# Attention steps levelled: projections in parts, score products chained, statistics spread, in a fused attention and top-p expert kernel

## The chip, the cores and the metric

One core of one Trainium2 chip runs the kernel. The metric is the device time of one execution in microseconds (us). Three executions of the kernel before were timed, and one more was profiled. TensorE multiplies matrices, VectorE and ScalarE work on rows of 128 partitions, GpSimd (POOL in the profile) does row work too and issues some of the DMAs, SyncE (SP) issues the others. "PEld" is TensorE's loading of weights. L557 is line 557 of the kernel before.

## What is computed

The input is 16 sequences of 256 tokens with 256 features. Each token is normalized; the result goes into 16-head attention (head size 16, rotary embedding, causal mask) and into eight experts, of which each token keeps those with the largest probabilities up to a sum of 0.9. Both results are added to the input.

```python
xn = layernorm(x)                                   # no scale, no shift
qkv = xn @ w_qkv.T + b_qkv;  q, k = rope(q), rope(k)
attn = softmax(where(causal, q @ k.T / 4, lowest)) @ v
p = softmax(xn @ router_w.T);  w = kept_top_p(p, 0.9)
ffn = sum_e( (silu(xn @ gate_w[e].T) * (xn @ up_w[e].T)) @ down_w[e].T * w[:, e] )
return x + attn + ffn
```

## The kernel before

All is in float32, and the work is in two stages with one order on TensorE.

**Attention stage.** A sequence is two tiles of 128 tokens. Its preparation consists of `prep_norm` (L419: normalize one tile on ScalarE, store it to `rows` in HBM through SyncE's queue, transpose it with two TensorE matmuls into `xnt`, copy to `xnT` on ScalarE), `prep_proj` (L434: matmuls `pq` for q and k and `pv` for v and the router's logits; VectorE adds the biases and does the rotary products in five operations at L445, L454, L465 to L467; GpSimd adds the halves into `qp` and `kp`, L468 and L471) and `prep_turn` (L475: four transposes of q or of k into `qt` or `kt`, then a ScalarE copy to `qT` or `kT`). Heads stand four to a group of 128 partitions, 32 partitions each, so that a product of one head uses 32 rows of TensorE.

The loop at L674 goes over steps. A step is two heads of one sequence, so that a sequence has eight steps (`PPS`), and there are 128. Step i makes the following:

- `products` (L532): the scores `s` of step i (queries by keys) and the transposed scores `st` of step i - 11 (`LAG`), each in two parts of two heads. Both write into buffers of the pool `ps_sc`, which has three in turn; `s` is allotted first.
- `probabilities` (L590): four mask matmuls into `st`, then one exponential on ScalarE (`pr`, L599), which empties the buffer of `st`.
- `maxima` (L564): four VectorE operations that reduce `s` to row maxima `top`, which empties the buffer of `s`. After the last step of a sequence `turn` transposes these and GpSimd adds them to `qT` (L588), where `st` of that sequence uses them.
- one job of the generator `prep_seq` (L639): one tile's norm, one tile's projection with rotation, or one transpose, in the order norm, norm, projection, projection, k, q, k, q.
- one tile of layer-norm sums (L399, L400) until all 32 are done, and at steps 7 and 31 `statistics` for the tiles that follow (square root on ScalarE, then two VectorE operations).
- from step 5 of every second sequence, six parts of the router for four tiles (L488), one in each step.
- every second step `weigh` (matmuls `o` of probabilities and v, copied to `oT` on ScalarE) and in the step after it `finish` (transposes `ot`, two VectorE operations, the sum into `xs` on GpSimd).

Everything that isn't a score goes through `ps_m`, a pool of two one-bank PSUM buffers in turn. Each engine runs its own queue in order. The order in the queue is not the order of the text: a scheduler makes it when the program is built, by priorities, and an instruction may stand ahead of others whose text came first. `issue_after` fixes that one instruction stands behind another.

**Before the loop** both sequences 0 and 1 are normalized and projected, and sequence 0 is turned. **After the loop** the experts run in groups of three blocks of tokens: gather by token number (L363), `expand`, `product`, and a scatter that adds into `out` (L809), both DMAs on GpSimd's queue. A ninth entry of the work, e = E, handles the block that didn't fit. `zero_fill` (L222), in step 24, clears the spare rows of `rows` and of `out` that unfilled places point to.

Of the kernel before, what the change touches and what calls it, by code (L numbers as in the profile page):

```python
# [30 lines left out]
def kernel(  # L31
# [68 lines left out]
    nc.vector.tensor_copy(ident_h, ident)  # L100
# [37 lines left out]
    for s in range(2):  # L138
# [4 lines left out]
    nc.gpsimd.memset(before, 1.0)  # L143
    nc.gpsimd.affine_select(
        before, before, pattern=[[1, E], [-1, E]], compare_op=ALU.is_gt, fill=0.0,
        base=0, channel_multiplier=0,
    )
    place = const.tile([P, E, E], F32, name="place")
    for k in range(E):
        nc.gpsimd.memset(place[:, k, :], float(k))  # L150
# [23 lines left out]
    zeros = const.tile([P, D + E], F32, name="zeros")  # L174

# [46 lines left out]
    def zero_fill():  # L222

        nc.gpsimd.memset(zeros, 0.0)
        nc.gpsimd.dma_start(
            rows[NT * P :, :].rearrange("(n p) c -> p n c", p=P),
            zeros.unsqueeze(1).to_broadcast([P, NB, D + E]),
        )
        nc.gpsimd.dma_start(
            out[NT * P :, :].rearrange("(n p) c -> p n c", p=P),  # L230
            zeros[:, :D].unsqueeze(1).to_broadcast([P, NB, D]),
        )
# [156 lines left out]
    with tc.tile_pool(name="prep", bufs=2) as prep, tc.tile_pool(  # L389
# [21 lines left out]
        seqs, stored, sums = {}, {}, {}  # L411
# [7 lines left out]
        def prep_norm(b, qi):  # L419

            t = b * NQ + qi
            xnT = seqs[b][3]
            xn = prep.tile([P, D], F32, tag="xn", name=f"xn_{t}", bufs=6)
            nc.scalar.activation(
                xn, xs[:, t, :], AF.Identity, bias=nmr[:, t : t + 1],
                scale=rstd[:, t : t + 1],
            )
            stored[b] = nc.sync.dma_start(rt[:, t, :D], xn)
            tp = ps_m.tile([P, DC, P], F32, tag="m", name=f"xnt_{t}")
            for c in range(DC):  # L430
                nc.tensor.transpose(tp[:, c, :], xn[:, ts(c, P)], ident)
            nc.scalar.copy(xnT[:, :, ts(qi, P)], tp)  # L432

        def prep_proj(b, qi):  # L434
# [12 lines left out]
            )  # L447
            pv = ps_m.tile([P, D + E], F32, tag="m", name=f"pv_{t}")
            for c in range(DC):
# [11 lines left out]

            cos = rope_sb[:, qi, 0, :].unsqueeze(1).to_broadcast([P, 2 * H, HD])
# [3 lines left out]
            nc.vector.tensor_tensor(rot[:, :, HF:], qk[:, :, :HF], sin[:, :, HF:], ALU.mult)  # L466
            nc.vector.tensor_tensor(qk, qk, cos, ALU.mult)  # L467
            nc.gpsimd.tensor_tensor(  # L468
                qp[b % 2][qi][:, :, :HD], qk[:, :H, :], rot[:, :H, :], ALU.add
            )  # L470
            sums[t] = nc.gpsimd.tensor_tensor(  # L471
                kp[b % 2][qi][:, :, :HD], qk[:, H:, :], rot[:, H:, :], ALU.add
# [59 lines left out]
        def products(now, late):  # L532
# [3 lines left out]
            for step, by_key in ((now, False), (late, True)):  # L536
                if step is None:
                    made.append(None)
                    continue
                b, c, p = step  # L540
                qT, kT, _, _ = seqs[b]
                sc = ps_sc.tile(
                    [P, 2, 512], F32, tag="sc", name=f"{'st' if by_key else 's'}_{b}_{c}_{p}"
                )
                made.append((kT if by_key else qT, qT if by_key else kT, c, p, sc, by_key))


            for first in (True, False):
                for left, right, c, p, sc, by_key in filter(None, made):
# [5 lines left out]
                    for j in range(2):  # L555
                        rows = slice(32 * (2 * p + j), 32 * (2 * p + j) + 32)
                        nc.tensor.matmul(  # L557
                            sc[:, j, to], left[rows, c, lhs],
                            right[rows, c, lhs if first else slice(0, S)],
                            start=first, stop=False, skip_group_check=True,  # L560
                        )
            return [m and m[4] for m in made]
# [76 lines left out]
        def prep_seq(b, turns_only=False):  # L639
            if not turns_only:  # L640
                for qi in range(NQ):
                    yield lambda qi=qi: prep_norm(b, qi)
                for qi in range(NQ):
                    yield lambda qi=qi: prep_proj(b, qi)
            for qi in range(NQ):
                yield lambda qi=qi: prep_turn(b, qi, "k")
                yield lambda qi=qi: prep_turn(b, qi, "q")
# [5 lines left out]
        stat_jobs = {7: (4, 8), 31: (12, 20)}  # L653
        stat_next = 2 * NQ

        for b in range(2):
            open_seq(b)
            for qi in range(NQ):
                prep_norm(b, qi)
            if b == 0:  # L660
                for qi in range(NQ):
                    prep_proj(b, qi)
        for qi in range(NQ):
            prep_proj(1, qi)
            prep_turn(0, qi, "k")
            prep_turn(0, qi, "q")
        with tc.issue_after(sums[2 * NQ - 1].ins):
            dispatch_constants()
# [4 lines left out]
        prs, jobs, held, todo = {}, None, {}, []  # L673
        for i in range(len(steps) + LAG + 5):  # L674
            if i < len(steps):
                b, c, p = steps[i]
                if i % PPS == 0 and b + 1 < B:
                    if b > 0:
                        open_seq(b + 1)
                    jobs = prep_seq(b + 1, turns_only=b == 0)  # L680
# [7 lines left out]
            if i < len(steps):  # L688
                behind = maxima(b, c, p, sc)
                if jobs is not None:  # L690
                    job = next(jobs, None)
                    if job is not None:
# [248 lines left out]
```

## Time and profile before

| | |
|---|---|
| median of three executions | 989.16 us (987.61 to 990.87) |
| the profiled execution | 983.91 us |
| its span, first to last instruction | 982.2 us |
| first matmul, first score product, first `st` | 6.80, 24.46, 48.31 us |
| step 12, step 120 begin | 52.16, 391.12 us |
| the last `st` burst begins | 435.48 us |
| mean granted TensorE clock | 0.984 |

The page gives each engine's busy time and share of the span, then the same in 40 equal slices in tenths, with the TensorE clock that was granted (PEclk, 9 is full). The list of waits says who waited for whom: the total in us, how often, and the longest. The instructions in order of time give start, duration, engine, line, and tiles as out<-in; a note in brackets is idle time before it and what ended it. Matmuls are pipelined, so they overlap in that list and their durations can't be added: the time that one takes up is from its start to the start of the next. In a table of stretches the columns are length, then busy us and number of instructions for PE, PEld, VectorE, ScalarE and GpSimd, then the granted clock, DMA share and GB/s.

### The profile page before, as it was taken

The page shows a single profiled execution, that of the slowest core. Times are in us where ns is not written, and L with a number is a line of the kernel's source. Part 1 is how long each engine was busy: PE and PEld are TensorE (multiplying, and loading weights), DVE is VectorE, ACT ScalarE, POOL GpSimd, SP SyncE. Part 2 cuts the span into 40 slices and gives each one's busy share as a digit, 9 for nine tenths or more (in the row PEclk, how much of TensorE's full clock was granted, in tenths as well). Part 3 has the DMA queues.
Part 4 walks back from the last instruction along what each step waited for, and adds up shares of the span by engine and source line. Part 5 has one row for each costly group of instructions (what it writes and reads, how often), then busy time and mean ns, then how long its engine had stood idle before and what let it go on. Part 6 is the DMA issues. An engine that isn't in the chain of part 4 may idle for free. (4 is left out here: it accounts for less than half of the span.)

```text
span 982.2 us, 17387 instructions
## 1 busy us (share of the span) xinstructions
PE 935.5 (95%) x6564; PEld 619.4 (63%) x6564; DVE 445.3 (45%) x2036; ACT 316.9 (32%) x617; POOL 393.7 (40%) x473
## 2 busy tenths in 40 slices
PE   6899999999999999899999999999999999999994
PEld 3555656565656565556676766766767677667673
DVE  6888676767676767825111244332111111121210
ACT  2544644444444443352222222222222222222221
POOL 6324333232323232424544444534544545546432
PEclk9799999999999999999999999999999999999997
DMA  7124100000020000102344242343433524335222
GB/s 242 42 69 154 44 18 27 21 23 24 23 82 23 13 12 13 44 14 56 54 94 74 44 114 34 55 102 55 91 67 49 119 45 91 69 54 95 41 27 28
DMA packets 46365, 57.53 MB, mean 59 GB/s; under 512 B 9312, under 2 KB 37600, under 8 KB 46272
## 3 DMA queue, kind: packets, MB, share of 16 engines
q0 software_dynamic: 19360, 29.81, 17.6%
q1 hardware_dynamic: 26912, 26.52, 8.5%
q8 instruction: 54, 0.88, 0.4%
q14 instruction: 39, 0.32, 0.1%
HBM read 32.14 MB, written 24.17 MB: 57 GB/s over the span
## 5 line engine op out<-in xcount | busy, mean ns | idle before, releaser
L809 POOL DMA_INDIRECT out<-ys,tokens x96 | 152.2, 1585 | 239.6 <-ACT ys L803 186.5
L763 DVE TENSOR_TENSOR hT<-act,gu 128x384 f32<-128x384 f32 (+2 forms) x132 | 69.9, 530 | 333.5 <-ACT act L762 333.5
L757 PE MATMUL gu<-xT,wg 128*128 128x384 f32 (+1 forms) x512 | 182.6, 479 | 1.4 <-DVE hT L763 1.0
L798 PE MATMUL py<-wd,hT 128*128 128x256 f32 (+1 forms) x768 | 182.4, 380 | 0.0
L570 DVE CUSTOM_DVE_ANT_0 junk<-s,mask 128x128 f32<-128x128 f32 (+1 forms) x512 | 152.9, 352 | 63.3 <-PE s L557 63.2
L757 PE MATMUL gu<-xT,wu 128*128 128x384 f32 (+1 forms) x512 | 179.8, 474 | 0.0
L798 PEld LDWEIGHTS py<-wd,hT 128*128 128x128 f32 (+1 forms) x768 | 141.7, 186 | 41.6 <-issue 3.8
L762 ACT ACTIVATE act<-gu 128x384 f32<-128x384 f32 (+2 forms) x132 | 62.2, 471 | 285.2 <-PE gu L757 285.2
L599 ACT ACTIVATE pr<-st 128x768 f32<-128x768 f32 x128 | 103.8, 811 | 154.9 <-PE st L594 154.9
L557 PE MATMUL s<-kT,qT 32*128 32x128 f32 (+1 forms) x1024 | 136.5, 366 | 3.7 <-DVE top L570 2.8
L557 PE MATMUL st<-qT,kT 32*128 32x128 f32 (+1 forms) x1024 | 125.3, 354 | 14.6 <-DVE top L570 11.8
L757 PEld LDWEIGHTS gu<-xT,wu 128*128 128x128 f32 x512 | 97.8, 191 | 61.5 <-issue 1.1
L757 PEld LDWEIGHTS gu<-xT,wg 128*128 128x128 f32 x512 | 89.8, 191 | 40.8 <-DVE hT L763 2.7
L363 POOL DMA_INDIRECT xg<-rows,tokens x96 | 94.2, 982 | 40.5 <-issue 20.4
L557 PEld LDWEIGHTS s<-kT,qT 32*128 32x128 f32 x1024 | 73.7, 188 | 33.6 <-issue 20.7
L557 PEld LDWEIGHTS st<-qT,kT 32*128 32x128 f32 x1024 | 69.2, 185 | 26.8 <-DVE top L570 22.4
L803 ACT ACTIVATE ys<-py,xg 128x256 f32<-128x256 f32 x96 | 45.4, 473 | 120.9 <-PE py L798 118.5
L630 POOL TENSOR_TENSOR xs<-xs,at 128x128 f32<-128x128 f32 x64 | 29.1, 455 | 128.4 <-DVE at L626 128.4
L468 POOL TENSOR_TENSOR qp<-qk,rot 128x256 f32<-128x256 f32 x32 | 23.5, 734 | 120.5 <-DVE qk L467 117.5
L440 PE MATMUL pq<-wqkv_sb,xnT 128*128 128x512 f32 x128 | 64.9, 631 | 0.0
L588 POOL TENSOR_TENSOR qT<-qT,topT 128x256 f32<-128x256 f32 x64 | 45.3, 739 | 41.5 <-ACT topT L586 41.5
L609 PE MATMUL o<-pr,va 128*32 128x256 f32 (+1 forms) x1024 | 58.1, 337 | 2.4 <-ACT xnT L432 0.6
(156 smaller groups left out, 916.6 us busy)
## 6 DMA issues: line engine op xcount, KB each, us to landing
rows<-xn SPq DMA_DIRECT2D x32, 128.0 KB, 1.8
wg<-in_wg SPq DMA_DIRECT2D x8, 512.0 KB, 4.0
wu<-in_wu SPq DMA_DIRECT2D x8, 512.0 KB, 5.0
wd<-in_wd SPq DMA_DIRECT2D x8, 512.0 KB, 3.9
out<-xs SPq DMA_DIRECT2D x16, 256.0 KB, 2.4
xs<-in_x SPq DMA_DIRECT2D x3, 1024.0 KB, 12.1
rows<-zeros POOLq DMA_DIRECT2D x1, 1716.0 KB, 8.1
out<-zeros POOLq DMA_DIRECT2D x1, 1664.0 KB, 12.4
```

The source lines that it names most:

```text
L363: nc.gpsimd.indirect_dma_start(out=xg[:n, :], out_offset=None, in_=rows, in_offset=bass.IndirectOffsetOnAxis(ap=token, axis=0),)
L440: nc.tensor.matmul(pq, xnT[:, c, ts(qi, P)], wqkv_sb[:, c, : 2 * D], start=(c == 0), stop=(c == DC - 1),)
L557: nc.tensor.matmul(sc[:, j, to], left[rows, c, lhs], right[rows, c, lhs if first else slice(0, S)], start=first, stop=False, skip_group_ch ...
L570: ins = nc.vector.tensor_tensor_reduce(junk[:, : hi - lo], sc[:, j, lo:hi], mask[:, 2 * P - (hi - lo) :], -1.0, -MASKED, ALU.add, ALU.min, ...
L599: nc.scalar.activation(pr, sc[:, :, :W], AF.Exp)
L609: nc.tensor.matmul(o[32 * hh : 32 * hh + 32, kc * P :], v[:, kc, 4 * c + hh, :], pr[:, j, : 2 * P] if kc == 0 else pr[:, j, 2 * P :], star ...
L757: nc.tensor.matmul(gu[:, j, :w], w_sb[:, c, ts(i, P)], xT[:, c, :w], start=(c == 0), stop=(c == DC - 1),)
L762: nc.scalar.activation(act[:, :w], gu[:, 0, :w], AF.Silu)
L763: nc.vector.tensor_tensor(hT[:, i, :w], act[:, :w], gu[:, 1, :w], ALU.mult)
L798: nc.tensor.matmul(py[:n, :], hT[:, i, k * P : k * P + n], d_sb[:, i, :], start=(i == 0), stop=(i == IC - 1),)
L803: nc.scalar.activation(ys[:n, :], py[:n, :], AF.Copy, scale=weights_of(e, xg, n))
L809: ins = nc.gpsimd.indirect_dma_start(out=out, out_offset=bass.IndirectOffsetOnAxis(ap=token, axis=0), in_=ys[:n, :], in_offset=None, compu ...
```

## The change

- `products` allots the buffer of `st` (the late step) ahead of that of `s`, and puts `st` ahead in each part. Every matmul of the burst but the first gets a higher priority and `issue_after` its forerunner.
- `prep_norm` handles both tiles of a sequence at once, with one PSUM tile and one copy. `prep_proj` is split into `prep_qk`, `prep_v` and `rotation`, which is a generator of two parts and does the k sum ahead of the q sum. A table `prep_jobs` says what each of the eight steps does: transposes and matmuls, and how many parts of rotations. Norm of a sequence is the last step two sequences ahead.
- Before the loop only sequence 0 is projected in full; sequence 1 has its norm and its first q and k projection there, and the rest in steps 0 to 7.
- One tile of layer-norm sums in every second step; `statistics` at steps 6, 22 and 54.
- The router's constants are made after the first kp and qp sums. The half-precision identity is copied by ScalarE instead of VectorE. `zero_fill` leaves out the last block of `out`; that one is cleared in the last entry of the expert work, behind a scatter of the last expert.

```diff
-    nc.vector.tensor_copy(ident_h, ident)
+    nc.scalar.copy(ident_h, ident)
...
-            for step, by_key in ((now, False), (late, True)):
+            for step, by_key in ((late, True), (now, False)):
...
-                        nc.tensor.matmul(
-                            sc[:, j, to], left[rows, c, lhs],
-                            right[rows, c, lhs if first else slice(0, S)],
-                            start=first, stop=False, skip_group_check=True,
-                        )
+                        with ExitStack() as hold:
+                            if opened is not None:
+                                hold.enter_context(tc.high_priority(offset=400))
+                                hold.enter_context(tc.issue_after(opened.ins))
+                            opened = nc.tensor.matmul(
+                                sc[:, j, to], left[rows, c, lhs],
+                                right[rows, c, lhs if first else slice(0, S)],
+                                start=first, stop=False, skip_group_check=True,
+                            )
...
-        def prep_norm(b, qi):
+        def prep_norm(b):
...
+            tp = ps_m.tile([P, NQ, DC, P], F32, tag="m", name=f"xnt_{b}")
+            for qi in range(NQ):
...
+            nc.scalar.copy(
+                xnT.rearrange("p c (q t) -> p q c t", q=NQ), tp
+            )
...
+        def rotation():
+            t, qk = unturned.pop(0)
...
             nc.vector.tensor_tensor(rot[:, :, :HF], qk[:, :, HF:], sin[:, :, :HF], ALU.mult)
             nc.vector.tensor_tensor(rot[:, :, HF:], qk[:, :, :HF], sin[:, :, HF:], ALU.mult)
+            yield
             nc.vector.tensor_tensor(qk, qk, cos, ALU.mult)
+            sums[t] = nc.gpsimd.tensor_tensor(
+                kp[b % 2][qi][:, :, :HD], qk[:, H:, :], rot[:, H:, :], ALU.add
+            )
             nc.gpsimd.tensor_tensor(
                 qp[b % 2][qi][:, :, :HD], qk[:, :H, :], rot[:, :H, :], ALU.add
             )
-            sums[t] = nc.gpsimd.tensor_tensor(
-                kp[b % 2][qi][:, :, :HD], qk[:, H:, :], rot[:, H:, :], ALU.add
-            )
...
+        def prep_jobs(b):
...
+            jobs = [
+                ([lambda: prep_qk(b, 0)] if b > 1 else [], 0),
+                ([lambda: prep_v(b, 0)], 1),
+                ([lambda: prep_qk(b, 1)], 1),
+                ([lambda: prep_v(b, 1)], 1),
+                (turn_of(0, "k"), 1),
+                (turn_of(0, "q") + turn_of(1, "k"), 0),
+                (turn_of(1, "q"), 0),
+                ([norm] if b + 1 < B else [], 0),
+            ]
...
-        stat_jobs = {7: (4, 8), 31: (12, 20)}
+        stat_jobs = {6: (4, 4), 22: (8, 8), 54: (16, 16)}
...
-                if jobs is not None:
-                    job = next(jobs, None)
-                    if job is not None:
-                        job()
+                todo_now, parts_now = jobs[i % PPS]
                 with tc.issue_after(behind.ins):
-                    if stat_next < NT:
+                    for _ in range(parts_now):
+                        if turning is None:
+                            turning = rotation()
+                        if next(turning, 0) == 0:
+                            turning = None
+                for job in todo_now:
+                    job()
...
+                with tc.issue_after(behind.ins):
+                    if stat_next < NT and i % 2 == 0:
...
-                        zero_fill()
+                        nc.gpsimd.memset(zeros, 0.0)
+                        zero_fill(rows, 0, NB)
+                        zero_fill(out, 0, NB - 1)
...
+                if e == E:
+                    with tc.issue_after(added[E - 1][-1]):
+                        ins = zero_fill(out, NB - 1, NB)
+                    for other in sum(added.values(), [])[:-1]:
+                        tc.declare_no_dep(ins.ins, other, reason="other rows")
+                    added[E - 1].append(ins.ins)
```

## The prediction, made before the changed kernel was run

> **What bounds the kernel now.** I read the page's busy shares, then the waits, then TensorE's instructions in order of time, step by step through the attention half, then two stretches that are one sequence each.
>
> ```profile
> PE 935.5 (95%) x6564; PEld 619.4 (63%) x6564; DVE 445.3 (45%) x2036; ACT 316.9 (32%) x617; POOL 393.7 (40%) x473
> PEclk9799999999999999999999999999999999999997
> ```
>
> TensorE is busy 95% of 982.2 us, so the end is set by what stands in its queue, and a gain has to show there. From about 450 us on (the experts) its order does not change. What can move lies in the first 440 us, and most of it inside what counts as busy.
>
> ```profile
> 200.91 0.38 PE L557 MATMUL s<-kT,qT 32*128 32x128 f32 x2
> 200.92 0.38 PE L557 MATMUL st<-qT,kT 32*128 32x128 f32 x2
> ...
> 201.77 0.40 PE L594 MATMUL st<-maskT_h,ident_h 128*128 128x128 bf16 x4
> ...
> 209.80 0.38 PE L557 MATMUL s<-kT,qT 32*128 32x128 f32 x2
> ...
> 233.78 0.49 PE L557 MATMUL s<-kT,qT 32*128 32x128 f32 x4
> 235.42 0.38 PE L557 MATMUL st<-qT,kT 32*128 32x128 f32 x2 [1.15 <-DVE top L570]
> 236.28 0.40 PE L594 MATMUL st<-maskT_h,ident_h 128*128 128x128 bf16 x4
> ```
>
> A step has a burst of sixteen 32-row matmuls: eight for s (step i) and eight for st (step i-11). The two use different 32-row groups. When both are ready they start together (first two lines) and the burst takes 201.77 - 200.91 = 0.86 us. Where eight run alone at the end of the stage (418.36 to 419.21) they take 0.85 us too: st is free if it is there in time. In the last three lines s runs alone, st comes 1.64 us late, and the burst takes 2.50 us.
>
> ```profile
> PEld st L557 <- DVE top L570: 22.4, 42, 1.7
> PE st L557 <- DVE top L570: 11.8, 16, 1.5
> 197.56:221.53 23.97, 23.64 (x271) 14.97 (x271) 16.06 (x85) 11.70 (x21) 7.40 (x12) 1.00 0.07 24
> 221.53:247.70 26.17, 24.32 (x271) 15.26 (x271) 19.40 (x98) 11.81 (x22) 7.40 (x12) 1.00 0.08 23
> ```
>
> The releaser of st is the maxima on VectorE: with three score buffers and s allotted first, st takes the buffer that s of the step before had, and waits for its four maxima. The two stretches are eight steps each, without and with the router (VectorE 16.06 and 19.40 us). Their eight bursts, from first score product to masks with foreign matmuls taken out, take 9.24 us (0.87, 0.87, 1.08, 1.03, 0.87, 1.43, 1.65, 1.44) and 11.42 us; whole they would be 8 x 0.87 = 6.95. So 2.29 and 4.47 us a sequence are lost, and the rest is the same in both: 23.97 - 2.29 = 21.68, and 26.16 - 4.47 = 21.69 (step 59 to 67 and on to 75). From step 12 (52.16 us) to step 120 (391.12) lie 13.5 sequences: 338.96 us, 25.1 each, 3.43 of them lost, 46 us in all.
>
> **The change, part by part.**
>
> *Late products allotted first, bursts chained.* By the allocation order st now takes the buffer of s two steps back, whose maxima are mostly long done: the wait above goes. What is late next: s takes the buffer of st of the step before, so s waits for that step's exponential on ScalarE. In the trace the exponential starts 0.43 us after the first mask matmul (421.41 to 421.84), takes 0.81, and TensorE follows a ScalarE copy about 0.06 later (26.15 to 26.21): s can start 1.30 us after its predecessor's masks begin. Masks hold TensorE for 0.23, so 1.07 us of other matmuls must stand between masks and the next burst. No row shows this wait; the nearest are late st: 0.23 late cost 1.08 - 0.87 = 0.21, 0.36 cost 0.56, 0.58 cost 0.57. I take these.
>
> *Preparation in parts.* No matmul is added or removed; they are spread. In the built order, with start-to-start times from the same stretch (pq 1.77, pv 0.95, o 0.79, kt 0.5, qt 0.44, four xnt 0.44, ot 0.33, top 0.32), what follows the masks is by step of the sequence: 0: pq, top 2.09. 1: pv, ot 1.28. 2: pq, o 2.56. 3: pv, ot 1.28. 4: kt, o 1.29. 5: qt, kt 0.94. 6: qt 0.44 (ot moved ahead of the masks). 7: xnt, ot 0.77 (o ahead of the masks). So steps 0 to 4 cover the exponential, barely in 1, 3 and 4 (0.2 us). After 5, s is 0.13 late: 0.2. After 6, 0.63: 0.6. After 7, 0.30, and the copy of o (0.37) stands ahead of the exponential, so about 0.49: 0.55. Sum 1.35, sequence 21.68 + 1.35 = 23.0.
>
> *The router sequence.* In step 3 the reductions r_m, r_p, the exponential on ScalarE and four more operations (1.4 us from 231.79 to 233.16, then 0.34) now stand on VectorE behind maxima, rotation half and v bias, and ahead of step 4's maxima and of the last rotation product. VectorE's queue, summed from step 2: step 3's maxima to 2.2 us after that burst begins, rotation and v 1.1, rs, at and router 1.9, step 4's maxima 1.2, product 0.6, then GpSimd's kp add 0.73: kp of the second tile comes 7.7 us, with the hand-overs some 7.9, after step 3's burst began, against 6.3 at which TensorE reaches its transpose in step 5. TensorE waits 1.6 us there, which covers step 5's 0.2. Behind that transpose stand step 6's burst and all else. Sequence 21.68 + 1.6 + 0.6 + 0.55 = 24.4. Bounds: 0.2 (VectorE catches up) to 3. Step 3's router exponential also stands ahead of step 4's on ScalarE; that 0.3 us lies within the 1.6.
>
> Gain per pair of sequences: (23.97 - 23.0) + (26.16 - 24.4) = 2.7; times 6.75 pairs, -18.2 us.
>
> *Statistics spread out.* VectorE has one tile in every second step instead of one in each (0.42 + 0.18 us busy): less in the first 24 steps, the same sum. But statistics now come at steps 6, 22 and 54, and 22 and 54 come just one step before the norm that needs them: square root, two VectorE operations, two norms (0.6 each), transposes, copy, then pq, with the next exponential between. The built order has three pairs of changes between the tables of square root and exponential after the start where there were two. Row: each load is 1.28 us (39.78, 47.54), so 2.6 for the added pair. The Trainium skill (ScalarE: Activation LUTs, What ACT_TABLE_LOAD costs) gives about 1283 ns for the load, which agrees, and about as much again for a drain, 2.66 in all, hence 5.3. The existing pair in step 33 lengthened its burst from 1.65 to 2.27 us only, since ScalarE is half idle. I take 2 us for each of 22 and 54, bounds 0 and 4: +4.
>
> *The start.* The first score product no longer stands behind pq and pv of sequence 1's second tile, its first pv and its first transposes. Before, it starts at 24.46 and its maxima at 26.96. By the same rows qT and kT of sequence 0 are ready near 22.6, so maxima start about 3.5 us earlier; 4.2 us of rotation and bias enter VectorE's queue in the eleven s-only steps and 2.6 of statistics leave. Then xnt, two pq and pv stand ahead of the first st, as one did before. I get step 12 at 49.4 instead of 52.16: -2.8, bounds -5 and +1; the upper depends on the clock, 0.5 from 36.5 to 46.7 us here. The cast of ident_h (5.30 us on VectorE at 5.94, beside GpSimd's fills) goes to ScalarE between norm and copy, where TensorE is waiting for nothing shorter: 0; uncovered it would be about 0.3. Router constants leave GpSimd's queue ahead of the first qp and stand behind kp and qp of sequence 0: 0, they are needed steps later. kp now goes ahead of qp: kT is used first, 0.
>
> *Joined xnT copies* (one instead of two): 0.2 us of ScalarE a sequence, off the path. *Zero fill*: two DMAs on GpSimd's queue stay in step 24, the second one block smaller; one of 128 KB is added behind the third last group's last scatter. It waits for that scatter's landing (3.8 us from issue, issue at 956.07), and the last group's scatters are queued behind it; the first went at 960.84, so perhaps 1 us late, the third, which the end follows, went at 966.21 after 1.21 idle: 0; without that cover about 1. SP's queue: the row stores keep their order: 0.
>
> **Sum.** -18.2 + 4 - 2.8 = -17.0. The profiled execution took 983.9 us (span 982.2); the median of three is 989.2, 0.5% above, so the difference is carried: 989.2 - 17.0 = 972.2, about 972.
>
> A rule that speaks against: the Trainium skill (TensorEngine Tiling (Array Packing), Performance Considerations) says packing speeds TensorE but not the emptying of PSUM, which may become the bound. Row: ScalarE 11.70 and VectorE 16.06 to 19.40 of 24 to 26 us, neither full. By full rate alone nothing would be lost (21.7 a sequence, -46 us); by the rule's letter all of it goes to emptying (0). My sum lies between, because the hand-over, not the rate, is late in three or four of eight steps.
>
> **Rivals.**
> *Bursts come out whole everywhere*: exponentials are in time and VectorE catches up. For it: neither engine is full. Against: 0.44 us of cover in step 6. -46 - 2.8 = 940. Chance 0.22, with what lies between it and mine (945 to 960).
> *The time moves from st to s and nothing is won*: 3.4 us of lateness a sequence, e.g. kp 3 us late in each pair and 0.8 a step for 6, 7, 0. 986 to 992, chance 0.08.
> *Slower*: a burst that cannot be split holds TensorE for all of ScalarE's delay. Place: steps 1, 3 and 4, whose cover is only 0.2 us. If kT, qT, oT or xnT copies (0.37 to 0.60) stand ahead of the exponential there too, it is 0.4 late in six steps: 2.4 more a sequence, 13.5 of them, +32 on 972, 1004. It decides from 17.0/13.5 = 1.3 us more a sequence. Against: in the built order these copies stand behind it in 3 and 4. Chance 0.12.
> *My sum*: 0.58.
>
> **Numbers.** What a measurement can tell from no change is about 0.3%, 3 us. Faster 0.80, same 0.08, slower 0.12. Range 945 to 987: it takes in the span of the start (6), of 22 and 54 (8), of the router wait (-10 to +9) and the upper part of the whole bursts; outside lie most of the slower case and the whole-burst end.
>
> **What would show it.** Right: st no longer waits for top; s waits for ACT pr after steps 5 to 7; kt waits for POOL kp in router sequences; sequences of 23.0 and 24.4 us; step 12 near 49. Wrong: bursts of 0.87 throughout (whole), or s waits in steps 1, 3, 4 (slower), or TensorE held at xnt around steps 24 and 56 for over 4 us.

## The result, and the profile after

| | before | after | forecast |
|---|---|---|---|
| median of the executions, us | 989.16 (987.6 to 990.9, 12) | 990.63 (975.4 to 1003.6, 12) | 972 (945 to 987) |
| after / before | | 0.991 (95%: 0.988 to 0.994) | 0.983 |

The ratio is made of the executions at 975 to 985 us; six others at 996 to 1004, the profiled one (1002.02) among them, ran at a lower mean granted TensorE clock (0.947 to 0.958 against 0.969 to 0.981). By this ratio the change gains 0.9%, about 9 us, where 17 were forecast. The median of all twelve shows no gain, and the kernel before stays within 5 us in each group of its executions: the spread of 28 us belongs to the change, as the part on the tail shows.

The profile's busy shares and granted clock after:

```profile
PE 940.4 (94%) x6564; PEld 615.4 (62%) x6564; DVE 455.9 (46%) x2037; ACT 317.0 (32%) x605; POOL 398.6 (40%) x474
PEclk9899899999999999557999999999999999999997
```

Two slices of the clock stand at 5 (about 400 to 450 us): the end of the attention stage. The middle of that stage came out shorter. One sequence with and one without the router, as stretches (length, busy us of PE, PEld, VectorE, ScalarE, GpSimd, clock):

```profile
229.55:253.85 24.30, 22.09 (x274) 13.70 (x271) 20.69 (x98) 11.54 (x21) 7.86 (x13) 1.00 0.08 24
253.85:276.14 22.29, 22.25 (x274) 13.89 (x270) 16.66 (x85) 11.44 (x20) 7.62 (x13) 1.00 0.30 96
```

They took 26.17 and 23.97. TensorE is busy all of the second, and idle for 2.2 us of the first. The waits of TensorE from 210 to 380 us say for what (total us, times, longest; the first line is the only one of the kernel before):

```profile
PE st L557 <- DVE top L570: 4.2, 6, 1.2
PE kt L495 <- POOL kp L481: 5.4, 4, 1.4
PE st L575 <- DVE top L589: 1.8, 3, 0.6
```

The wait at kt is the one forecast at 1.6 us. Set against the profile before by stretches (start of the first score product of a step, `s` or `st`, to that of another), with clean sequences (those without statistics) of 22.29 and 24.30:

| stretch | before | after | difference | forecast |
|---|---|---|---|---|
| to step 12 | 52.16 | 52.93 | +0.8 | -2.8 |
| 6.75 pairs of clean sequences | | | -23.8 | -18.2 |
| excess of steps 20 to 28 and 52 to 60 | | 34.81, 29.22 | +10.5, +4.9 | +2, +2 |
| rest up to step 120 | | | -0.4 | 0 |
| step 120 to the last `st` | 44.36 | 68.04 | +23.7 | 0 |
| experts | 546.7 | 549.2 | +2.5 | 0 |
| span | 982.2 | 1000.3 | +18.1 | -17.0 |

Step 12 to 120 is 338.96 before, 330.14 after. Two things need explaining: 15 us at two statistics, and 24 us in the tail.

### The profile page after: what moved, and what is told of

Read it like the earlier page. It is cut to its first block, busy times and chain, and to the rows that moved or that the text cites. A ratio compares the mean times of both kernels' runs of the same rounds, so it can differ in the third digit from the quotient of the medians.

```text
span 1000.3 us, 17417 instructions
## 1 busy us (share of the span) xinstructions
PE 940.4 (94%) x6564; PEld 615.4 (62%) x6564; DVE 455.9 (46%) x2037; ACT 317.0 (32%) x605; POOL 398.6 (40%) x474
## 3 DMA queue, kind: packets, MB, share of 16 engines
q0 software_dynamic: 19376, 29.81, 17.1%
q1 hardware_dynamic: 26912, 26.52, 8.3%
## 4 chain that ended last, share of the span: by engine, by line
PE 83%; DVE 12%; ACT 2%; DMA 1%; issue 1%; POOL 0%; POOLq 0%; DVEq 0%; ACTq 0%
PE gu L798 32%; PE py L839 17%; PE st L575 8%; PE pq L442 6%; PE o L628 5%; DVE junk L589 3%; PE st L613 3%; PE s L575 2%; PE xt L784 2%; PE pv L458 2%; PE ot L640 1%; PE qt L495 1%; DVE less L328 1%; PE xnt L431 1%; PE kt L495 1%
## 5 line engine op out<-in xcount | busy, mean ns | idle before, releaser
L575 PE MATMUL st<-qT,kT 32*128 32x128 f32 (+1 forms) x1024 | 137.5, 382 | 5.7 <-DVE top L589 5.7
L575 PE MATMUL s<-kT,qT 32*128 32x128 f32 (+1 forms) x1024 | 121.3, 360 | 6.5 <-DVE top L589 4.2
L575 PEld LDWEIGHTS st<-qT,kT 32*128 32x128 f32 x1024 | 75.8, 202 | 30.4 <-issue 17.1
L575 PEld LDWEIGHTS s<-kT,qT 32*128 32x128 f32 x1024 | 68.5, 191 | 17.2 <-issue 7.8
L628 PE MATMUL o<-pr,va 128*32 128x128 f32 (+1 forms) x1024 | 65.0, 363 | 4.9 <-ACT topT L605 2.7
L607 POOL TENSOR_TENSOR qT<-qT,topT 128x256 f32<-128x256 f32 x64 | 47.9, 779 | 51.8 <-ACT topT L605 51.8
L628 PEld LDWEIGHTS o<-pr,va 128*32 128x32 f32 x1024 | 29.2, 117 | 44.2 <-issue 22.2
```

The lines of the kernel that those rows point to most:

```text
L575: opened = nc.tensor.matmul(sc[:, j, to], left[rows, c, lhs], right[rows, c, lhs if first else slice(0, S)], start=first, stop=False, skip ...
L607: nc.gpsimd.tensor_tensor(qT[:, c, :], qT[:, c, :], topT, ALU.add)
L628: nc.tensor.matmul(o[32 * hh : 32 * hh + 32, kc * P :], v[:, kc, 4 * c + hh, :], pr[:, j, : 2 * P] if kc == 0 else pr[:, j, 2 * P :], star ...
```

## Experiments

Each line of the tables below comes from the run's own profile; times are compared with runs of the kernel before on the same chip (984.0 to 985.9 us there).

### What happens at step 22

ScalarE's instructions after, from 85 to 99 us:

```profile
85.05 1.28 ACT L404 ACT_TABLE_LOAD   x1
87.67 0.30 ACT L404 ACTIVATE std<-mv,eps_sb 128x8 f32<-128x8 f32 x1 [1.33 <-DVE mv L399]
...
88.25 1.28 ACT L618 ACT_TABLE_LOAD   x1
89.54 0.81 ACT L618 ACTIVATE pr<-st 128x768 f32<-128x768 f32 x1
90.25 1.57 ACT L425 ACTIVATE xn<-xs,nmr,rstd 128x256 f32<-128x256 f32 x3
91.86 0.58 ACT L432 COPY xnT<-xnt 128x512 f32<-128x512 f32 x1
92.34 0.82 ACT L618 ACTIVATE pr<-st 128x768 f32<-128x768 f32 x1
93.04 1.57 ACT L425 ACTIVATE xn<-xs,nmr,rstd 128x256 f32<-128x256 f32 x3
97.69 1.09 ACT L425 ACTIVATE xn<-xs,nmr,rstd 128x256 f32<-128x256 f32 x2 [3.08 <-DMA rows<-xn]
98.69 0.35 ACT L605 COPY topT<-top 128x256 f32<-128x256 f32 x1
```

The prediction counted two norms; there are eight. The statistics make eight tiles ready at once, and the scheduler put the norms of sequences 5, 6 and 7 behind those of 4. There are six buffers, so the seventh waits 3.08 us for the store of the first, with the copy `topT` queued behind it, and TensorE behind that:

```profile
99.09 1.06 PE L628 MATMUL o<-pr,va 128*32 128x256 f32 x2 [2.70 <-ACT topT L605]
```

The clock then stands at 0.5 from 98.8 to 105.7 us. What the store met is in the DMA rows from 80 to 100 us (KB of each, median us from issue to landing):

```profile
rows<-zeros POOLq DMA_DIRECT2D x1, 1716.0 KB
out<-zeros POOLq DMA_DIRECT2D x1, 1536.0 KB
rows<-xn SPq DMA_DIRECT2D x8, 128.0 KB, 4.5
```

`zero_fill` of step 24 was issued at 82.99 and 84.36 us, and when the norms are stored the DMA engines are full (a share of 1.02 from 88 to 96 us). The stores there take 4.5 us in the median, where the quickest transfers of this run to `rows` take 1.7. So the norms of step 22 probably meet a DMA that the prediction put at 0; no run moved it, and its share is not shown.

The first theory: the norms in a row are the loss.

**Norms held at their own step** (`e1_norms_held`; `emptied` is the list of exponentials).

```diff
-                nc.scalar.activation(xn, ...)
+                with ExitStack() as hold:
+                    if emptied:
+                        hold.enter_context(tc.issue_after(emptied[-1].ins))
+                    nc.scalar.activation(xn, ...)
```

> The changed kernel, with each norm on ScalarE made to stand behind the last exponential ahead of its own step, so that norms of later sequences can't be moved up to the statistics at steps 22 and 54. Theory (hoisted norms): the loss at 22 and 54 comes from eight norms in a row on ScalarE and from the wait of the seventh for the store of the first (3.08 us), not from the table loads. Then steps 20 to 28 take 25 to 27 us (34.81 in the changed kernel), steps 52 to 60 25 to 26.5 (29.22), the clock of 0.5 at 99 us is gone, and the time of undisturbed executions falls by 9 to 13 us, from 975 to about 964. Rival (table loads): the load of 1.28 us and its pair stay, so the two stretches stay within 3 us of what they were. The spread of 975 to 1003 between executions should stay by both.

Measured: slower than before, 999.8 us (ratio 1.0145, 1.009 to 1.020). Steps 20 to 28 took 28.24, 1.2 above what the theory wanted, but 52 to 60 stayed at 29.21, and every other sequence grew, to 24.79 and 26.53. ScalarE shows why, around step 80:

```profile
271.63 0.82 ACT L621 ACTIVATE pr<-st 128x768 f32<-128x768 f32 x1
272.33 1.09 ACT L428 ACTIVATE xn<-xs,nmr,rstd 128x256 f32<-128x256 f32 x2
273.95 0.58 ACT L435 COPY xnT<-xnt 128x512 f32<-128x512 f32 x1 [0.53 <-PE xnt L434]
274.43 0.82 ACT L621 ACTIVATE pr<-st 128x768 f32<-128x768 f32 x1
```

Norm, transposes and copy now stand in one chain between two exponentials, and the bursts of steps 80, 81 and 82 take 1.49, 1.27 and 1.27 us instead of 0.87. In the changed kernel the norms run one sequence or more ahead, and that is worth 2.2 to 2.5 us a sequence. The theory falls as stated: norms ahead are no loss, they carry a good part of the gain. What it leaves is a split of the 4.9 us at step 54: with norms held, that sequence is 29.21 - 26.53 = 2.7 us over its like (the tables and the chain to the norm), and 26.53 - 24.30 = 2.2 is what is lost when norms are not ahead, as those of a sequence whose statistics have only just come can't be. The split itself is argued; that all 4.9 come from the late statistics is shown further down.

**Eight buffers instead of six** (`e9_eight_buffers`; with the chain cut as in `e2_tail_open` below).

```diff
-                xn = prep.tile([P, D], F32, tag="xn", name=f"xn_{t}", bufs=6)
+                xn = prep.tile([P, D], F32, tag="xn", name=f"xn_{t}", bufs=8)
```

> The changed kernel with the chain cut at step 118 and eight buffers instead of six for normalized tiles, so that the seventh norm at step 24 doesn't wait for the store of the first. Base: the run with the chain cut, steps 20 to 28 34.74 us, 52 to 60 29.21, 977.5 us. Theory (the wait for the store is the largest part): the idle of 3.1 us on ScalarE and the 2.7 us at o on TensorE go, and with them the dip of the clock at 98.7 us (6.8 us at half clock, 3.4 us): 20 to 28 takes 28 to 30 us, and the time is 971 to 974. 52 to 60 has ten norms in a row instead of eight and stays or rises by up to 1. Rival (norms in a row are the cost, waiting or not): 20 to 28 falls by less than 2.

Measured: 20 to 28 takes 28.98, 52 to 60 29.29. In that profile the five norms that follow one another take 2.56 us without a wait, and neither the 2.7 us at `o` nor the dip of the clock appears. The median, 975.0, fell only by 2.5 from 977.5, and the ratio is the same (0.9905 for both), so the 5.8 us that the stretch gained in the profile are not shown in the time: the executions of each differ by 4 to 6 us.

**One sequence ahead, no more** (`e10_one_ahead`; chain cut, six buffers): as in `e1_norms_held`, but `if len(emptied) > 8` and `emptied[-9]`.

> The changed kernel with the chain cut at step 118 and each norm held behind the exponential of eight steps earlier than its own step, so that norms run at most one sequence ahead: four in a row at steps 23 and 55 instead of eight. Statistics as changed. Base as before: 34.74, 29.21, 977.5 us. If the norms in a row are the cost, 20 to 28 falls to 26.5 to 28.5 us (24.3, the 1.7 that the statistics cost where each norm was held at its own step, and two norms of 0.6), 52 to 60 to 26 to 28; the other sequences keep 22.3 and 24.3, since the gain of having norms ahead (2.5 us a sequence, the difference to the run with norms held) needs one sequence only. In all 967 to 971. If more than one sequence ahead is what helps, the others rise towards 24.8 and 26.5.

Measured: the other sequences keep 22.30 and 24.30, so one sequence ahead is enough. But 52 to 60 stays at 29.21 with four norms in a row as with eight, and 20 to 28 takes 32.06, with the clock at 0.5 from 92.6 to 99.4 us though nothing waited for a store: 3.1 us above the run with eight buffers, which had no such dip. Median 975.3, not 967 to 971. So the number of norms in a row costs nothing by itself.

Why the clock fell in one run and not in another can be read from the traces. In each of them all falls and returns lie on one grid of 3.41 us, which begins at another time in each run. The waits of TensorE near 90 us are the same in `e9_eight_buffers`, `e10_one_ahead` and `e11_dense_work` (further down; up to here it is the changed kernel), but they lie differently on the grid. The last piece of it before 93 us, first in `e11_dense_work`, then in `e9_eight_buffers`, and the piece with the wait behind `topT` in the changed kernel:

```profile
89.01:92.42 3.41, 1.69 (x18) 1.21 (x19) 1.33 (x11) 3.40 (x5) 0.00 (x0) 1.00 1.01 361
88.68:92.10 3.42, 2.06 (x24) 1.47 (x24) 1.34 (x10) 3.37 (x6) 0.00 (x0) 1.00 1.02 367
95.42:98.83 3.41, 0.97 (x11) 0.66 (x9) 1.70 (x5) 1.14 (x3) 0.00 (x0) 1.00 0.61 207
```

With TensorE busy for 1.69 us (1.74 in `e10_one_ahead`) or 0.97 of 3.41, a fall follows; with 2.06 it does not. That is no threshold: ahead of the fall at 446.1 us of the kernel before it was 2.38. And `e11_dense_work`, whose ScalarE waits 3.05 us for the store as in the changed kernel, takes 32.05 for steps 20 to 28, as `e10_one_ahead` does without that wait: at half clock TensorE is busy through it. So of the 10.5 us at step 22, 4.7 remain in `e9_eight_buffers` without store wait and fall, 3.1 come with a fall, and 2.7 with the store wait where no fall stood ahead of it. The 4.7 are close to the 4.9 of step 54. What remains is that the statistics come too late.

**Statistics early** (`e8_stats_early`, chain cut).

```diff
-        stat_jobs = {6: (4, 4), 22: (8, 8), 54: (16, 16)}
+        stat_jobs = {6: (4, 6), 27: (10, 22)}
...
-                    if stat_next < NT and i % 2 == 0:
+                    if stat_next < NT:
```

> The changed kernel with the chain cut at step 118 and with the layer-norm sums in every step again, statistics at steps 6 (six tiles) and 27 (all the rest), four steps ahead of their first norm. Theory (statistics too late): steps 20 to 28 (34.7 us with the chain cut) lose 10.5 us and steps 52 to 60 (29.2) lose 4.9 because the statistics come one step ahead of the norm that needs them, with up to eight norms at once. Then 20 to 28 and 52 to 60 fall to 24.3 to 25.5 us, 28 to 36 rises by 0 to 3 from its 22.2, and the time is 961 to 967 against 977.5. Rival (it's the amount of hoisted norms, wherever it comes): five to six norms in a row at step 27 cost the same again there, 28 to 36 takes 27 to 33 us, and the time stays above 970.

Measured: 968.6 us, ratio 0.984 (0.981 to 0.986), 1.6 above what the theory said. 52 to 60 is 24.29: all of the 4.9 gone. 20 to 28 is 26.63, 28 to 36 25.26; but 12 to 20 rose from 23.19 to 26.60, where `st` waited 1.4 us for the maxima and the clock fell to 0.5 from 56.1 to 63.0 us (half of these 6.8 us is the whole rise). That sums in each step are the reason is not shown: the next run makes them in each step from 13 on, and 12 to 20 stays at 23.18.

**Statistics at 18 and 34** (`e12_stats_18_34`: chain cut, norms one sequence ahead).

```diff
+        stat_jobs = {6: (4, 4), 18: (8, 8), 34: (16, 16)}
...
+                    if stat_next < NT and (i % 2 == 0 or i > 12):
```

> The changed kernel with the chain cut at step 118, norms at most one sequence ahead, and the statistics moved from steps 22 and 54 to 18 and 34 (sums in every second step up to step 12, then in every step), so that each comes at least five steps ahead of its first norm. By the theory that the late statistics cost 4.9 us each (2.2 to 2.5 because that sequence's norm can't run ahead, 1.7 to 2.7 for the table loads and the chain to the norm), and the rest of 20 to 28 is the wait for a store and the clock, 20 to 28 falls from 34.7 to 24.5 to 26, 52 to 60 from 29.2 to 24.3, 12 to 20 and 28 to 36 rise by 0 to 2 each for the loads; 963 to 967 us against 977.5, and 0 to 5 below the run with statistics at 6 and 27 (968.6). Rival (a square root among the exponentials costs about 3 us wherever it stands): 12 to 20 takes 26 and 28 to 36 25.5, and the time is 968 to 971.

Measured: 964.3 us, ratio 0.980 (0.977 to 0.983). 12 to 20 23.18, 20 to 28 25.57, 28 to 36 22.57, 52 to 60 24.29. The two stretches that now hold the square roots, 12 to 20 and 28 to 36, are 0.0 and 0.3 us above the same ones of the changed kernel (23.19, 22.22): the rival is out. Norms held and sums moved as well, so the run is not one edit; but in `e10_one_ahead` the same hold alone left 52 to 60 at 29.21. This is the fastest kernel of the study:

```profile
PE 909.5 (95%) x6564; PEld 600.4 (62%) x6564; DVE 455.6 (47%) x2037; ACT 317.2 (33%) x605; POOL 399.1 (41%) x474
PEclk9799999999999999899999999999999999999997
```

With the same 6564 instructions TensorE is busy 30.9 us less than in the changed kernel's profile, some 20 of them in the tail, where no slice of the clock is below 8.

### The tail

After step 119 the counting and finding of tokens (`first`, `seen`, `part`, L248 to L336) shares the score buffers: `seen` takes them from `ps_sc`, so not everything but scores goes through `ps_m`, as the first part has it. Stretches of the changed kernel, then TensorE's longest wait there:

```profile
396.00:400.00 4.00, 2.31 (x22) 0.97 (x18) 3.96 (x25) 0.00 (x0) 2.47 (x4) 0.90 0.35 101
404.00:408.00 4.00, 4.00 (x34) 2.07 (x32) 0.92 (x7) 0.96 (x2) 1.19 (x2) 0.50 0.26 68
430.00:440.00 10.00, 10.00 (x72) 5.93 (x64) 1.00 (x4) 3.17 (x5) 0.76 (x2) 0.50 0.01 2
398.80 0.38 PE L575 MATMUL s<-kT,qT 32*128 32x128 f32 x2 [1.69 <-DVE part L324]
```

TensorE is idle for 1.7 of 4 us (half an `st` is out, the `s` chained to it waits for `part` on VectorE), and at 399.2 the clock falls to 0.5. From then on TensorE counts as busy for all but 0.2 us, and the clock stays there for 58.0 us, until the experts' matmuls. A burst of eight `st` takes 1.58 us instead of 0.86. The low clock is all that is lost: in `e1_norms_held`, chained throughout too, step 120 to the last `st` took 48.3 us, 10.2 of them at half clock, which by estimate (time at half clock counted half) is 43.2 at full clock. The kernel before took 44.4 with 3.4 at half clock, 42.7 by the same estimate.

**Chain cut at step 118** (`e2_tail_open`).

```diff
-                            if opened is not None:
+                            if chain and opened is not None:
```

(`chain` is true in steps with `i < 118`)

> The changed kernel, with the score products chained in steps 0 to 117 only; from 118 on (the last ones, with the dispatch work between them) they are free again. Theory (held bursts): st that was issued early and s that waits for VectorE's dispatch work leave TensorE idle from 388 to 400 us, the clock falls to 0.5 and doesn't come back in the tail of 32-row products. Unchained, idle time there falls by 2 to 4 us, the tail's bursts take 0.86 instead of 1.58, and executions of about 1003 us disappear: all lie between 970 and 985. Rival (the dispatch itself): idle time comes from the waits for order, holds and part, which the kernel before had too; then the spread of 975 to 1003 stays.

Measured: 977.5 us (972.6 to 979.0), ratio 0.9905 (0.987 to 0.994). The steps ahead of 118 are as in the changed kernel. The same stage in its profile:

```profile
400.00:404.00 4.00, 4.00 (x38) 1.98 (x34) 3.31 (x21) 0.72 (x2) 2.46 (x3) 0.50 0.26 72
414.00:424.00 10.00, 10.00 (x128) 6.26 (x125) 2.55 (x14) 6.24 (x10) 4.10 (x7) 1.00 0.01 2
```

The clock falls here too, at 395.7, after idle time of the same size (`s` for `part` 1.4 us, where it was 1.7), but it comes back at 409.3: the idle time didn't shrink as expected, only what follows changed. With the chain cut none of 24 executions (this run, `e3_held_and_open`, `e8`, `e9`, `e10`, `e12`) lies more than 7 us above the fastest of its kernel; with the chain throughout, the changed kernel spreads by 28, and `e1_norms_held` by 28 as well (`e7_no_chain`, below, by 11). The chain alone does not decide it: in the profiles of `e1_norms_held`, `e5_swap_chain` and `e6_now_first`, all chained throughout, the longest fall in the tail lasted 6.8, 20.5 and 13.7 us.

**Norms held and chain cut** (`e3_held_and_open`): the edits of `e1_norms_held` and `e2_tail_open` together.

> Norms held behind their own step's exponential, and no chain from step 118 on: both edits together. If they act in different places the gains add: 962 to 967 us in nearly all executions, against 975 to 1003 of the changed kernel and 989 of the one before. If the spread is not due to the chain, single executions of 985 and above remain.

Measured: 994.7 us (992.1 to 997.6). Held norms cost what they cost alone (sequences of 24.79 and 26.52); the spread is gone.

**Dense work in the tail** (`e11_dense_work`, chain throughout).

```diff
+            if len(steps) <= i < len(steps) + 3:
+                warm = ps_m.tile([P, 512], F32, tag="m", name=f"warm_{i}")
+                for w in range(8):
+                    nc.tensor.matmul(warm, wqkv_sb[:, 0, :P], wqkv_sb[:, 1, :512],
+                                     start=(w == 0), stop=(w == 7))
```

> The changed kernel (chain everywhere) with 24 added matmuls of 512 columns in full float32, eight in each of the first three steps that have only st; nobody reads them. At full clock they take about 24 x 0.5 = 12 us, at half clock twice that. Theory (the tail stays at half clock because 32-row products, though they keep TensorE busy, don't count as enough work to raise it): dense work raises the clock, the T-only bursts after it take 0.86 in every execution, so that no stretch of half clock lasts from 399 to 457 us; the spread between executions falls from 28 us to less than 15, and the time is 986 to 1000. Rival (what lowers the clock is outside TensorE's work, so it comes back by itself after some time): bursts stay at 1.58 after the added work in an execution that had them before it, and times reach 1010 to 1030.

Its stretches, and the instructions where the clock comes back:

```profile
415.00:420.00 5.00, 5.00 (x24) 2.49 (x24) 1.52 (x11) 0.81 (x1) 0.45 (x1) 0.50 0.01 3
420.00:425.00 5.00, 5.00 (x20) 2.46 (x19) 0.84 (x6) 0.81 (x1) 0.00 (x0) 0.99 0.00 0
```

```profile
416.10 1.91 PE L720 MATMUL warm<-wqkv_sb 128*128 128x512 f32 x2
...
420.06 0.92 PE L575 MATMUL st<-qT,kT 32*128 32x128 f32 x8
420.92 6.28 PE L720 MATMUL warm<-wqkv_sb 128*128 128x512 f32 x14
...
445.66 0.92 PE L575 MATMUL st<-qT,kT 32*128 32x128 f32 x8
```

The clock had been at 0.5 from 392.8; the first of the added matmuls ran from 416.1 to 418.0, at 420.1 the clock was back, before the other 23 began, and it stayed: the bursts with only `st` take 0.86. The added work takes 21 us (7.13 for eight at full clock), not 12: such a matmul is two records of 0.44 us. The four executions lie at 997 to 1006, a spread of 9 instead of 28, and none at the 1020 that the low clock and the added work would make together. The spread agrees with the theory and not with the rival; three of the four times lie between the ranges of both, since the added work was sized too small. But there is one profile of it, and the clock also came back without added work, with the chain cut and in the three chained runs named above; that this one matmul raised it is possible and not shown.

### Which part makes the sequences shorter

**Late products first, alone** (`e4_swap_only`, on the kernel before) and **with the chain** (`e5_swap_chain`); **the changed kernel with `s` allotted first** (`e6_now_first`) and **without the chain** (`e7_no_chain`).

```diff
-            for step, by_key in ((now, False), (late, True)):
+            for step, by_key in ((late, True), (now, False)):
```

(the reverse in `e6_now_first`; in `e7_no_chain` the condition ahead of the two `enter_context` is `False`)

> The kernel before, with one edit: the late products are allotted their buffer first and stand first in each part. Preparation, statistics and chaining as before. If the order of allotment is the main part of the gain, st's wait for the maxima goes (22 us of it in the weight loads and 12 in the matmuls) and a sequence gets 1 to 1.7 us shorter, 965 to 977 us in all. If the preparation in parts is what makes room for the exponential, s waits for the exponential of the step before in the steps with only one transpose behind the masks, 1 us and more in two or three steps of eight, and the time stays within 985 to 993.

> The kernel before with the late products first (as in the run with that edit alone) and with each burst chained; preparation and statistics as before. The edit alone gave sequences of 23.77 and about 26.4 us, the kernel before 23.97 and 26.16, the changed kernel 22.29 and 24.30. If the chain brings the gain, the sequences come down to 22.3 to 23 and 24.3 to 25 us. If the preparation in parts brings it, they stay at 23.5 to 24.5 and 26 to 27.5, since the chain only moves the wait for the exponential from the middle of a burst to its start.

> The changed kernel with the buffer of s allotted first again and s first in each part; parts, chain and statistics as changed. If the order of allotment carries the gain of the sequences, st waits for the maxima of the step before, and since the burst is chained it waits whole: 0.3 to 1.2 us a step where VectorE has more in its queue, sequences of 24 to 26 us without and 26 to 29 us with the router. If the parts alone carry it, they stay within 0.3 us of 22.29 and 24.30.

> The changed kernel without chain and without the raised priority of the burst, all else as changed. If the chain matters only in the last sequence (where it did harm), sequences stay within 0.3 us of 22.29 and 24.30, the tail runs at the full clock, and the time is that of the run with the chain cut at step 118: 973 to 979. If the chain is what keeps the bursts whole, bursts of 1.2 to 2.5 us come back, sequences take 23 to 24.5 and 25 to 26.5 us, and the time is 985 to 1000.

| | parts | late first | chain | without router | with router | us (before there) |
|---|---|---|---|---|---|---|
| before | | | | 23.97 | 26.15 | |
| `e4_swap_only` | | x | | 23.77 | 26.4 to 27.9 | 988.0 (984.4) |
| `e5_swap_chain` | | x | x | 23.26 | 25.9 and 26.9 | 985.7 (985.9) |
| `e6_now_first` | x | | x | 22.06 | 26.0 to 27.4 | 988.5 (985.9) |
| `e7_no_chain` | x | x | | 22.98 | 25.63 | 998.7 (985.9) |
| after | x | x | x | 22.29 | 24.30 | |

No single edit carries the gain. Allotment alone is 0.3% slower (1.001 to 1.005). From 52 to 390 us `st` waits 0.3 us for the maxima instead of 11.3, but `s` waits 3.0 for exponentials, and most of all `o` waits for `at` on VectorE, 8.8 us in five waits. The parts bring the sequences without the router down by whichever order of allotment; there `s` first is even 0.2 us better. In those with the router VectorE is late, and with `s` allotted first TensorE waits in the same 170 us as above:

```profile
PE st L575 <- DVE top L589: 9.7, 6, 2.6
```

where the changed kernel has 1.8. The chain with its raised priority is worth 0.7 and 1.3 us a sequence, more than expected, and without it the two statistics cost more (37.2 and 37.3 us for steps 20 to 28 and 52 to 60, each with a fall of 17.1 us, which is 8.5 of them). Chain and priority were not tried apart, and the parts without chain and with `s` first were not run. These are stretches of one profile each; `e5` and `e6` were executed once, so their total times say little.

## Why the prediction was right, and where it was wrong

**The total: right way and within the range, in part by luck.** Up to step 120 the sum came out at -8.0 and not -17.0: the sequences gained 5.6 us more than forecast, the statistics lost 11.4 more, the start 3.6 more. Errors of opposite sign met, and the tail, which had no term, puts the median of all executions (990.63) outside the range.

**The mechanism of the sequences: right, its sum too small.** `st`'s wait for the maxima went from 4.2 to 1.8 us in 170; kt waits for kp 1.4 a time (forecast 1.6). `s` was to come late in three places. After step 6 it does:

```profile
262.77 0.49 PE L575 MATMUL st<-qT,kT 32*128 32x128 f32 x4
263.30 0.38 PE L575 MATMUL s<-kT,qT 32*128 32x128 f32 x2
```

The exponential of the step before runs from 262.43 to 263.24, `s` starts 0.06 later, and the burst takes 1.38 instead of 0.87: 0.5, forecast 0.6. After step 5 `s` is in time (forecast 0.2). After step 7 nothing is lost (forecast 0.55): there the step that failed is "s takes the buffer of st of the step before". That buffer is free only when the exponential is done, and `s` starts in the middle of it:

```profile
265.40 0.82 ACT L618 ACTIVATE pr<-st 128x768 f32<-128x768 f32 x1
265.94 0.38 PE L575 MATMUL s<-kT,qT 32*128 32x128 f32 x2
```

The semaphores that the trace records with the first `s` are ScalarE's in steps 1 and 3 to 7, but VectorE's in steps 0 and 2: in those the buffer came from an earlier `s`. So 22.29 instead of 23.0, and 24.30 instead of 24.4: 5.6 us more gain than forecast. For the sequences without the router the rival of whole bursts (21.68) was about as near as the sum (23.0); for those with it (24.30 measured) it was wrong: VectorE does not catch up, and kt waits.

**Statistics: the term that failed.** "I take 2 us for each of 22 and 54, bounds 0 and 4", measured 10.5 and 4.9. The costs that the prediction named (tables, square root, two operations, norms) are of the size it gave: 2.7 at step 54 with norms held. What it missed is that the norms elsewhere run a sequence ahead and here can't (2.2), and at 22 the eight norms on six buffers: the wait for a store, probably slow behind `zero_fill`, holds ScalarE (2.7 on TensorE), and a fall of the clock follows (6.8 us at half speed, about 3). It also left out that the square root itself waits 1.33 us for the last tile of sums (line 87.67 above). A row for many norms at once was in the profile before, at step 7, one step ahead of the norm; of eight norms these are seven:

```profile
42.10 1.09 ACT L424 ACTIVATE xn<-xs,nmr,rstd 128x256 f32<-128x256 f32 x2 [0.73 <-DVE nmr L407]
44.95 2.57 ACT L424 ACTIVATE xn<-xs,nmr,rstd 128x256 f32<-128x256 f32 x5
```

Instead the statistics in step 31 were taken as the row for it; they come nine steps ahead of their norm. The Trainium skill's price of a table load (ScalarE: Activation LUTs, What ACT_TABLE_LOAD costs) was the larger of the two figures weighed. Of the drain in it these lines show nothing: the load from 88.25 ends at 89.53, and the exponential starts at 89.54. Run `e12` has the same two table pairs five steps or more ahead of their norms, and steps 12 to 20 and 28 to 36 stay at 23.18 and 22.57: the price of the load isn't the point, its distance from the norm is.

**The start: wrong.** -2.8 was forecast, +0.8 came. The first score product did come 2.2 us earlier (22.26). But what had stood ahead of it (`pv`, `pq`, `pv`, four transposes) went in among the eleven s-only steps, where kt waits 1.74 us for kp and `s` 1.44 for maxima, and step 10 is at 39.39 (39.00 before): the same work stands between the same ends.

**The tail: not forecast at all.** The sum ends at step 120 and puts nothing for what follows, without a reason. But the chain acts on bursts there too, with the dispatch between them. That the spread of 28 us goes when the chain is cut is shown, by two kernels with it and six without. That a long low clock like the profiled one makes the other long executions is likely by their mean clocks, but only one of them was profiled; why it lasts there is open. The slower rival (held bursts in steps 1, 3 and 4) did not happen: those bursts take 0.87.

**Zero fill, xnT join, ident_h, the ends of SP and GpSimd:** 0 was forecast; with the chain cut the time from the last `st` to the end is 545.2 us (546.7 before, with 3.4 us at half clock in it, so 545.0). At step 24 `zero_fill` was probably not free (above).

## What to carry to other kernels

When a step is moved next to the step that needs it, count what the scheduler had been able to run ahead of time, and read the order of each engine's queue for how many instructions become ready at once, how many buffers they have, and which DMA is under way then. A burst that may not be split saves time where everything arrives evenly, and should be limited to there: where foreign work waits in between, it passes each delay on to TensorE whole. If the time of a kernel spreads while that of its forerunner didn't, look at the granted clock of the profile first.

## What the runs showed of the hardware

- A busy TensorE need not get its clock back. From 404 to 450 us the changed kernel's TensorE is 100% busy with 32-row products and fewer 128-row ones, at a clock of 0.50. The Trainium skill (TensorE: Matmul & The Clock Gate, Part 1) has the clock return after about one busy window of 3.4 us; here it stayed low for 58.0 us, 17 times that, and the measurement decides. In `e11_dense_work` the return came 2.1 us behind one matmul of 512 columns on all 128 rows (two records, 1.9 us); whether that matmul brought it is open.
- Apart from the one at the end of the span, the falls last 3.41, 6.83, 10.24, 13.65, 17.1, 20.5, 27.3 and 58.0 us in these traces, all multiples of 3.41, as that section's window says, and in one trace all lie on one grid. Whether the same waits bring one on depends on how they lie on it: those near 90 us did with 1.69 and 1.74 us of busy time in one piece of 3.41, and did not with 2.06.
- An instruction is not always where its text is: norms moved one sequence ahead by the scheduler were worth 2.2 to 2.5 us in 22 to 24.
